# Attention and a two-layer graph convolution on one core: square-block transposes by VectorE and DMA, a Strassen form for two more groups, and half of x's operand sums later

## The chip, the cores and the metric

The kernel runs on one core of a Trainium2 chip. A core has four compute engines that run side by side: TensorE (PE, matrix products), VectorE (DVE), ScalarE (ACT) and GpSimd (POOL). A fifth, SyncE (SP), issues DMA transfers only. Each engine works through its own queue of instructions in order, and waits in it for semaphores of the others. The metric is the device time in microseconds of one execution of the whole kernel; lower is better. Beside the times there is one profiled execution, of which everything below is read.

## The reference

All is float32; there are N = 4096 nodes, x has D = 512 columns, `adj` is 4096 x 4096, the hidden width is H = 128.

```python
# layer 0: attention with adj added twice to the scores
q = x @ Wq.T + bq;  k = x @ Wk.T + bk;  v = x @ Wv.T + bv
a = q @ k.T / sqrt(D) + adj + adj
x = layernorm(x + softmax(a) @ v)
# layer 1: two graph convolutions
h = relu(adj @ (x @ W1) + b1)
out = adj @ (h @ W2) + b2
x = layernorm(x + out)
```

## The kernel before, in words

**Layer 0.** The queries are cut into NG = 8 groups of W = 512 rows, each of PER = 4 row tiles of 128. Queries and keys are never formed by themselves: with M = Wq.T Wk the scores of a group are u.T x, where u is a 512 x 512 operand of the group, made once by `u_products` (plain, sixteen products of 512 columns) or by `u_fast` (Strassen's form). For each group the 4096 keys are taken in 8 blocks d of 512. In Strassen's form after Winograd a block's scores are seven half-size products instead of eight, taken in the order 1, 2, 6, 7, 5, 4, 3 (`qk`), each of two halves j; their operands on the side of x are plain pieces of x.T or sums that were stored to DRAM (`SA`, loaded by `load_s` into the 8 slots of the pool `sap`). Two PSUM banks, X and Y, take the products, and `qk_read` (L449) adds a bank to the scores `S` on DVE: X after products 1, 6, 5, 3, Y after 2, 7, 4. The product 7 opens bank Y anew, so it must wait until DVE has read what product 2 left there. Into `S` goes beforehand a row constant (`begin_scores`, ACT) and adj, by an accumulating DMA on POOL's queue (`add_scores`, L385).

When all of a group's scores are there, they are reduced by their maximum (`shift`, L479, DVE), exponentiated (L483, ACT), summed to the denominator (L489, L492, POOL), and turned into Strassen operands (L519 and L520 on POOL, L526 and L531 on DVE). Then P x, the weights times x, follows in five ranges of key pairs with the same seven products (`px_items`, L576): 224 products a group. Their x operands `xn` are plain pieces of x, or sums of x's quarters that `sum_x` forms on POOL (L364 to L367) from rows that it loads on SP, sixteen times q, and stores as `xs_d`; for q of 2 and more it also takes two row sums of x on DVE (L408). `load_x` fetches an `xn` three phases ahead. P x is read from PSUM by `px_read` (L547 on ACT, L549 on DVE).

**The row stage.** What P x of group g - 1 gave is finished beside P x of group g and the scores of group g + 1: `row_items` (from L754) lists the steps. First V's product with P x: for groups in `FAST_V` (0 to 5) by Strassen, `rows_out_fast`, 28 products of 256 columns, with four operand sums on DVE; for groups 6 and 7 `rows_out`, 16 products of 512 columns. Then layer norm (`rows_norm`), giving the rows x1 in `XR[:, r]`, and for each tile r of 128 rows:

- `add_b2` (L732, L734): POOL adds b2 into a tile `xb`, which takes a slot of the pool `sap`, and stores it to DRAM (`x_d` in the profile) from POOL's queue, for the end of layer 1;
- `project` (L740 to L742): four PE transposes of 128 x 128 into a PSUM bank, and an ACT copy to `x1t`, of which there is one buffer (a tile of V's Strassen sums, `s3`, shares it);
- `project2` (L749, L752): four products x1 W1, and a DVE copy into `t_sb`, where all of x1 W1 is kept for layer 1.

**Layer 1** runs after that, also by Strassen, then in plain parts at the end; the change doesn't touch it.

**Order.** The order of the work is written by hand. The main loop goes through units; one has seven places, two units are a block d of the scores. At each place PE gets a product half of `qk`; hooks put there by `at(unit, place, f)` run before it; then as many steps of the unit's work list (`work[...]`) follow as their estimated PE times allow. The work list of units 33 to 48 (and so on every 16) is the row stage of group g - 1 with the products of P x of group g interleaved: `w(n)` in `row_items` stands for n products of P x. In the first units the work list holds the making of u for the groups to come, and the hooks hold the forming of x's operands, `m_sums` and `m_t3` (operands of u's Strassen form) and `sum_x`. SP's queue carries, in order of issue, the loads of `sa`, of `xn`, of `ut` and of the rows for `sum_x`; POOL's queue carries the accumulates of adj and the stores of `xs_d`, of u and of x1, each behind POOL's arithmetic.

## Time and profile before

| what | value |
|---|---|
| time, median of 3 runs (range) | 2304.09 us (2303.28 to 2306.04) |
| the profiled execution | 2308.84 us |
| its span | 2307.1 us |
| PE busy | 2276.3 us, 99% |
| DVE busy | 1617.0 us, 70% |
| POOL busy | 1018.7 us, 44% |
| ACT busy | 399.8 us, 17% |
| DMA packets, bytes | 282711, 525.14 MB |

A line of a group of instructions names the line of the kernel, the engine, the operation, output and inputs by the program's names, shapes and count, then busy time and the mean of one, then the idle time ahead of it on its engine and what ended it. Busy times of PE overlap one another, so the cost of a product is the distance from its start to the next start. In a timeline each line is a run of instructions: start, duration, engine, line; a bracket at its end gives idle time ahead and the releaser. A window's line gives start and end, length, then busy time and number of instructions of PE, PEld (the loads of PE's weights), DVE, ACT and POOL, then PE's granted clock as a share of full speed, the busy share of the DMA engines, and GB/s. Lines of DMA issues give the number, the size of one and the median time from issue to landing.

### The profile page before, as it was taken

What the parts mean: (1) busy time and instruction counts of PE and PEld (TensorE: products, weight loads), DVE (VectorE), ACT (ScalarE), POOL (GpSimd) and SP (SyncE); (2) the same over time, 40 slices, a digit from 0 to 9 for tenths busy, and PEclk for the clock granted to TensorE, in tenths of its full rate; (3) what the DMA queues carried; (4) which work ended last, traced back from release to release, by engine and by line L of the source; (5) the groups of instructions that cost most, each with busy time, mean ns of one, the idle gap of its engine ahead of it and who ended that gap; (6) DMA issues with size and microseconds to landing.
All of it is one profiled execution on the core that took longest, in us unless ns stands there. A gap on an engine that the chain in (4) does not pass through costs nothing.

```text
span 2307.1 us, 28475 instructions
## 1 busy us (share of the span) xinstructions
PE 2276.3 (99%) x10672; PEld 1750.6 (76%) x10672; DVE 1617.0 (70%) x2276; ACT 399.8 (17%) x438; POOL 1018.7 (44%) x1009
## 2 busy tenths in 40 slices
PE   9999999999999999999999999999999999999998
PEld 5888788888888888888888888888876743333456
DVE  4676776687667756765776687568657877888864
ACT  2212211131122112111311121122102000000012
POOL 3565654185327424731653274237429830001043
PEclk9999999999999999999999999999999999999999
DMA  6999878667857684777578586947754468899996
GB/s 177 273 284 309 233 215 230 193 174 215 246 135 218 189 246 114 215 213 215 151 221 232 145 218 193 259 117 210 196 191 155 155 237 321 332 347 375 352 383 218
DMA packets 282711, 525.14 MB, mean 228 GB/s; under 512 B 23184, under 2 KB 130448, under 8 KB 281680
## 3 DMA queue, kind: packets, MB, share of 16 engines
q1 hardware_dynamic: 229040, 406.12, 52.3%
q0 software_dynamic: 43296, 105.39, 20.7%
q10 hardware_dynamic: 10240, 11.82, 1.7%
q8 instruction: 85, 1.39, 0.2%
q14 instruction: 50, 0.41, 0.0%
HBM read 475.27 MB, written 46.41 MB: 226 GB/s over the span
## 4 chain that ended last, share of the span: by engine, by line
PE 92%; DVE 4%; POOL 2%; DMA 1%; issue 1%; ACT 0%; SPq 0%; POOLq 0%; DVEq 0%; ACTq 0%
PE p L576 32%; PE X L436 18%; PE b L1041 15%; PE Y L436 14%; PE v L703 3%; PE acce L1342 2%; PE psu L234 2%; PE ops L1296 1%; PE tps L749 1%; PE psu L262 1%; PE x L651 1%; PE x1ps L740 1%; DVE s L449 1%; PE psm L856 1%; DMA u_d<-uo 1%
## 5 line engine op out<-in xcount | busy, mean ns | idle before, releaser
L576 PE MATMUL p<-s,xn 128*128 128x256 f32 x3584 | 895.6, 380 | 7.0 <-DVE s L531 2.6
L576 PEld LDWEIGHTS p<-s,xn 128*128 128x128 f32 x3584 | 677.1, 190 | 111.0 <-DVE s L531 5.6
L436 PE MATMUL X<-ut,sa 128*128 128x256 f32 x1984 | 513.4, 381 | 1.7 <-DVE s L449 1.7
L492 POOL TENSOR_TENSOR lacc<-lacc,s 128x512 f32<-128x512 f32 x240 | 344.1, 1434 | 203.2 <-ACT s L483 192.3
L436 PEld LDWEIGHTS X<-ut,sa 128*128 128x128 f32 x1984 | 370.1, 190 | 64.2 <-DVE s L449 15.3
L449 DVE TENSOR_TENSOR s<-X,s 128x512 f32<-128x512 f32 x256 | 176.3, 689 | 278.6 <-PE X L436 278.2
L436 PE MATMUL Y<-ut,sa 128*128 128x256 f32 x1408 | 361.6, 380 | 0.2 <-DVE s L449 0.2
L436 PEld LDWEIGHTS Y<-ut,sa 128*128 128x128 f32 x1408 | 266.8, 190 | 37.7 <-issue 1.4
L483 ACT ACTIVATE s<-s 128x1024 f32<-128x1024 f32 x128 | 135.3, 1057 | 790.3 <-DVE s L479 790.3
L458 DVE TENSOR_TENSOR macc<-macc,s 128x512 f32<-128x512 f32 x240 | 258.1, 1075 | 1.2
L449 DVE TENSOR_TENSOR s<-Y,s 128x512 f32<-128x512 f32 x192 | 131.9, 687 | 157.0 <-PE Y L436 155.7
L479 DVE TENSOR_TENSOR s<-s,mb 128x512 f32<-128x512 f32 x256 | 231.2, 913 | 2.4 <-ACT mb L399 2.4
L385 POOL DMA_DIRECT2D s<-in_adjT_dram x64 | 84.4, 1318 | 256.7 <-ACT s L380 255.9
L549 DVE TENSOR_TENSOR ot<-p,ot 128x512 f32<-128x512 f32 x248 | 168.9, 681 | 31.4 <-PE p L576 31.2
L1008 DVE TENSOR_TENSOR tt<-ck 128x1024 f32<-128x1024 f32 x112 | 138.4, 1270 | 38.7 <-PE b L1041 33.6
L1041 PE MATMUL b<-tt,st 128*64 128x512 f32 (+1 forms) x768 | 156.0, 541 | 0.0
L380 ACT COPY s<-cb 128x2048 f32<-128x2048 f32 x64 | 121.0, 1890 | 48.1 <-PE p L576 39.8
L519 POOL TENSOR_TENSOR s<-s 128x256 f32<-128x256 f32 x128 | 124.6, 974 | 0.6
L1041 PEld LDWEIGHTS b<-tt,st 128*64 128x64 f32 x768 | 53.9, 137 | 87.8 <-issue 79.9
L526 DVE TENSOR_TENSOR s<-s 128x512 f32<-128x512 f32 x128 | 114.3, 914 | 0.0
L520 POOL TENSOR_TENSOR s<-s 128x256 f32<-128x256 f32 x128 | 107.8, 842 | 10.0
L489 POOL TENSOR_TENSOR lacc<-s 128x512 f32<-128x512 f32 x8 | 10.6, 1321 | 197.9 <-ACT s L483 197.9
(186 smaller groups left out, 2112.6 us busy)
## 6 DMA issues: line engine op xcount, KB each, us to landing
ck<-in_adjT_dram SPq DMA_DIRECT2D x128, 1024.0 KB, 7.4
s<-in_adjT_dram POOLq DMA_DIRECT2D x64, 1024.0 KB, 11.5
sa<-s_d SPq DMA_DIRECT2D x224, 256.0 KB, 5.7
xn<-in_x_dram SPq DMA_DIRECT2D x192, 256.0 KB, 4.3
xn<-xs_d SPq DMA_DIRECT2D x96, 512.0 KB, 5.7
sa<-in_xT_dram SPq DMA_DIRECT2D x168, 256.0 KB, 4.7
xn<-xs_d SPq DMA_DIRECT2D x64, 256.0 KB, 3.9
ut<-u_d SPq DMA_DIRECT2D x49, 256.0 KB, 7.2
```

Source lines behind the costliest of these rows:

```text
L380: nc.scalar.copy(s, CB[g].unsqueeze(1).to_broadcast([P, 4, W]))
L436: nc.tensor.matmul(T["X" if k in (1, 6, 5, 3) else "Y"][:, ts(j, HW)], SA[g, d, a][:, c, j, :], UT[g, b][:, c, :], start=k in (1, 2, 7) an ...
L449: nc.vector.tensor_tensor(ck, ps, ck, ALU.add)
L458: nc.vector.tensor_tensor(MACC[g], MACC[g], ck[:, h, :], ALU.max)
L479: nc.vector.tensor_tensor(ck, ck, MB[g], ALU.subtract)
L483: nc.scalar.activation(ck, ck, AF.Exp, scale=2.0)
L492: nc.gpsimd.tensor_tensor(LACC[g], LACC[g], ck[:, h, :], ALU.add)
L519: nc.gpsimd.tensor_tensor(b12, b12, b11, ALU.subtract)
L549: nc.vector.tensor_tensor(to, ps, to, ALU.add)
L576: nc.tensor.matmul(T["PX" if k in (1, 6, 5, 3) else "PY"][:, ts(f, HW)], XN[n][:, q - a, ts(f, P)], quarters(g, q)[{1: 0, 2: 2, 6: 1, 7: 0 ...
L1008: nc.vector.tensor_tensor(t[:, :2], v[:, :, 1], v[:, 0], ALU.subtract)
L1041: nc.tensor.matmul(BK[n][k][ts(half, HH)], lhs, right(u, i, half, b), start=q == 0, stop=q == NP - 1,)
```

## The change

There are five edits.

1. For groups 0 to 5, `project` gives way to three steps for each tile. `turn_blocks`: one DVE transpose of `XR[:, r]` into `x1t`, which transposes each 32 x 32 block in its place. `store_blocks`: four DMAs on SP's queue, which write `x1t` to DRAM (`xt_d`) with the blocks exchanged, in runs of 32 values. `load_blocks`: one DMA on SP's queue, which reads `xt_d` back into `XR[:, r]`, over the rows that it came from; `project2` then takes its x1 from there. The order of the row stage's steps is new, and `add_b2` comes earlier in it.
2. `FAST_V` takes in group 6. For this group alone the four operand sums are on POOL, and `project` of tile 2 comes two products of P x later.
3. u of group 1 is made by `u_fast` like those of groups 2 to 7, and their work list runs over units 1 to 15 instead of 3 to 15. `m_sums` and `m_t3` move to unit 0; one of the operands and `g_t` change places in memory.
4. `sum_x` for the sixteen q: units 0 to 15 become 0, 2, 4, 6, 8, 10, 12, 14, 15, 16, 18, 20, 21, 22, 24, 25.
5. The scores of block 1 of group 0 are begun at places 0 and 1 of unit 0 instead of 4 and 5.

```diff
+    xt_d = {
+        (g, r): dram.tile([P, ND, P], F32, name=f"xt_d{g}_{r}")
+        for g in range(NG - 2)
+        for r in range(PER)
+    }
...
-    g_t = mp.tile([P, D], F32, name="g_t")
-    ms_t = mp.tile([P, 2, 2, HW], F32, name="ms_t")
+    g_t = t_sb[:, NT - PER :, :].rearrange("p a b -> p (a b)")
+    ms_t = mp.tile([P, 3, 2, HW], F32, name="ms_t")
...
-    FAST_V = range(NG - 2)
+    FAST_V = range(NG - 1)
...
-        MV[T1] = t_sb[:, 28:32, :].rearrange("p (c a) b -> p c (a b)", c=2)
-        MV[T2], MV[T4] = (ms_t[:, n] for n in range(2))
+        MV[T2], MV[T4], MV[T1] = (ms_t[:, n] for n in range(3))
...
+        sum_ = (nc.gpsimd if g == NG - 2 else nc.vector).tensor_tensor
...
-            tt(T["s3"], a11, a21, ALU.subtract)
-            tt(a21, a21, a22, ALU.add)
+            sum_(T["s3"], a11, a21, ALU.subtract)
+            sum_(a21, a21, a22, ALU.add)
...
-                tt(a11, a21, a11, ALU.subtract)
+                sum_(a11, a21, a11, ALU.subtract)
...
-                tt(a12, a12, a11, ALU.subtract)
+                sum_(a12, a12, a11, ALU.subtract)
...
+    def turn_blocks(g, r):
+        T["x1t", g, r] = rowp.tile([P, ND, P], F32, tag="x1t", name=f"x1t{g}_{r}")
+        nc.vector.transpose(T["x1t", g, r].rearrange("p c i -> p (c i)"), XR[g][:, r, :])
+
+    def store_blocks(g, r):
+        x1t = T.pop(("x1t", g, r))
+        to = xt_d[g, r].rearrange("(b i) c (a j) -> a i c b j", i=32, j=32)
+        for a in range(4):
+            nc.sync.dma_start(
+                to[a], x1t[ts(a, 32)].rearrange("i c (b j) -> i c b j", j=32)
+            )
+
+    def load_blocks(g, r):
+        T["x1t", g, r] = XR[g][:, r, :].rearrange("p (c i) -> p c i", i=P)
+        nc.sync.dma_start(T["x1t", g, r], xt_d[g, r])
...
+        if g < NG - 2:
+            turn, store, load = (
+                lambda r, f=f: [item(0, f, g, r)] for f in (turn_blocks, store_blocks, load_blocks)
+            )
+            return [
+                *(item(0.86, rows_out_fast, g, k, j) for k in ORDER for j in range(2)),
+                *w(1), item(0, rows_last, g), *norm(2), *norm(3), *w(4), *turn(2), *w(2), *store(2),
+                *norm(0), *b2(2), *w(2), *norm(1), *w(6), *turn(3), *load(2), *b2(3), *w(2),
+                *store(3), *w(8), *turn(0), *load(3), *b2(0), *w(2), *store(0), *pro2(2), *w(8),
+                *turn(1), *load(0), *b2(1), *w(2), *store(1), *pro2(3), *w(8), *load(1), *w(2),
+                *pro2(0), *w(8), *pro2(1),
+            ]
...
-                *w(1), item(0, rows_last, g), *norm(2), *norm(3), *w(2), *pro(2), *w(2), *pro(3),
+                *w(1), item(0, rows_last, g), *norm(2), *norm(3), *w(2 + 2 * (g == NG - 2)), *pro(2), *w(2),
+                *pro(3),
...
-    work[0] = 3, [(0.86, f) for f in u_products(1)]
-    work[3] = 13, [(0.86, f) for g in range(2, NG) for f in u_fast(g)] + [(0, lambda: owing.pop()())] * 2
-    at(1, 0, m_sums)
-    at(3, 0, m_t3)
+    work[1] = 15, [(0.86, f) for g in range(1, NG) for f in u_fast(g)] + [(0, lambda: owing.pop()())] * 2
+    at(0, 0, m_sums)
+    at(0, 1, m_t3)
...
-    for q in range(NP):
-        at(max(q - 1, 0), 0, sum_x, q)
+    for q, u in enumerate((0, 2, 4, 6, 8, 10, 12, 14, 15, 16, 18, 20, 21, 22, 24, 25)):
+        at(max(u - 1, 0), 0, sum_x, q)
         for r in range(2):
-            at(q, 2 + 3 * r, lambda q, r: T["sum_x", q][0](r), q, r)
-        at(q, 6, lambda q: T["sum_x", q][1](), q)
-        at(q + 1, 2, lambda q: T["sum_x", q][2](), q)
+            at(u, 2 + 3 * r, lambda q, r: T["sum_x", q][0](r), q, r)
+        at(u, 6, lambda q: T["sum_x", q][1](), q)
+        at(u + 1, 2, lambda q: T["sum_x", q][2](), q)
...
-                at(s0 + q - early, 4, begin_scores, g, d)
-                at(s0 + q - early, 5, add_scores, g, d)
+                place = 0 if s0 + q == early else 4
+                at(s0 + q - early, place, begin_scores, g, d)
+                at(s0 + q - early, place + 1, add_scores, g, d)
```

## The prediction

> **What bounds the kernel now.** The engine totals first, then the chain that ended last:
>
> ```profile
> span 2307.1 us, 28475 instructions
> PE 2276.3 (99%) x10672; PEld 1750.6 (76%) x10672; DVE 1617.0 (70%) x2276; ACT 399.8 (17%) x438; POOL 1018.7 (44%) x1009
> ...
> PE 92%; DVE 4%; POOL 2%; DMA 1%; issue 1%; ACT 0%; SPq 0%; POOLq 0%; DVEq 0%; ACTq 0%
> ```
>
> TensorE is busy throughout and carries 92% of the chain. Every PE product taken out is worth its interval, as long as no new wait reaches PE; every wait that reaches PE costs its length. So two things are wanted: intervals, and margins. The PE timeline in a group's row stage gives the intervals (start, duration; the next start counts, since matmuls overlap):
>
> ```profile
> 473.28 0.60 PE L740 MATMUL x1ps<-ident,xr 128*128 128x128 f32 x4
> 473.71 1.03 PE L436 MATMUL Y<-ut,sa 128*128 128x256 f32 x4
> 474.58 1.03 PE L576 MATMUL p<-s,xn 128*128 128x256 f32 x4
> 475.44 1.05 PE L749 MATMUL tps<-w_t,x1t 128*128 128x128 f32 x8
> 476.33 1.03 PE L436 MATMUL X<-ut,sa 128*128 128x256 f32 x4
> ```
>
> Four transposes cost 473.71 - 473.28 = 0.43 us; two 256-column products (x4 records) 0.87, so 0.433 each; project2 0.89. By stages (window, length, busy PE, PEld, DVE, ACT, POOL, then clock, DMA share, GB/s):
>
> ```profile
> 100.00:150.00 50.00, 47.86 (x211) 40.69 (x211) 34.50 (x54) 9.45 (x16) 31.42 (x34) 0.97 1.00 269
> 280.00:320.00 40.00, 38.74 (x175) 32.58 (x175) 34.38 (x41) 6.07 (x6) 24.55 (x21) 1.00 0.89 244
> 720.00:740.00 20.00, 19.94 (x91) 16.92 (x91) 18.18 (x21) 2.85 (x2) 17.84 (x16) 1.00 0.86 249
> ```
>
> A row stage keeps DVE and POOL at 90% of 20 us with PE unhindered, so its waits are met with little to spare. The first 320 us are the only place before layer 1 with real PE losses: summing PE's start-to-start excess over each form's interval gives 10.2 us in 100 to 243, 3.8 in 243 to 320, and only 11.5 in all of 430 to 1600. DMA is full there. What a loss looks like:
>
> ```profile
> 143.77 1.13 PE L234 MATMUL psu<-xt,ms_t 128*128 128x256 f32 x4 [1.91 <-ACT uo L211]
> 144.74 1.80 PE L436 MATMUL Y<-ut,sa 128*128 128x256 f32 x4
> 146.33 1.91 PE L234 MATMUL psu<-xt,ms_t 128*128 128x256 f32 x4
> ```
>
> 1.91 us idle, then 3.4 us at half pace (granted clock 0.97 over that window): such a stall costs another 1.7 us.
>
> **What the skill says.** "TensorE: Matmul & The Clock Gate", What's actually happening: the gate goes to half rate after an idle window of about 3.4 us; the trace agrees on the 3.4 us of half pace, and shows it after 1.91 us idle already, so I charge 1.7 us to stalls near 2 us. "VectorE: DVE Perf Modes", The TRN2 errata: an f32 tensor_tensor takes (N+151)/0.96 ns, 691 at N = 512; the eviction row of the trace has 689 (L449). The three transpose paths: VectorE's transpose makes independent 32x32 blocks, so the blocks' places must be moved by something else, here the DMA. "DMA: Bandwidth & Descriptors", Specifications: under 512 B a transfer falls off the line rate, with a read-modify-write; the new stores have 128 B runs and no row of the trace has such.
>
> **The change part by part.**
>
> *1. Transposes of groups 0 to 5.* Removed: 24 sets of four transposes, 24 x 0.43 = 10.3 us of PE; with them 24 copies of 0.59 us on ACT, which idles. Added per tile: one VectorE block transpose of 128x512; four SP DMAs writing 256 KB as 2048 runs of 128 B; one SP load of 256 KB. The transpose has no row: 0.69 us by the nearest (f32 128x512, skill 0.691), up to 1.4 if it runs at half that rate, as the 128x512 rows beside POOL do (L458, 1.075); 24 x 0.69 = 16.6 us hidden in DVE's idle 10% or more, and under its floor there is no gain to bound. Issue of a DMA on SP about 0.45 us.
>
> What matters is the new order of waits. add_b2 moves ahead of most of the products of P x, since its x1 rows must be read before the load overwrites them. In every row stage (times after its first P x product, 676.74 for group 1) POOL is still working until +14.7:
>
> ```profile
> 686.13 2.95 POOL L492 TENSOR_TENSOR lacc<-lacc,s 128x512 f32<-128x512 f32 x2
> 689.04 1.18 POOL L519 TENSOR_TENSOR s<-s 128x256 f32<-128x256 f32 x1
> 690.30 1.12 POOL L520 TENSOR_TENSOR s<-s 128x256 f32<-128x256 f32 x1
> ...
> 706.38 1.77 POOL L732 TENSOR_TENSOR xb<-xr,b_t 128x512 f32<-128x512 f32 x1
> 708.45 0.63 POOL L734 DMA_DIRECT2D x_d<-xb  x1 [0.30 <-POOL xb L732]
> ```
>
> I laid the new order out by its intervals. (a) add_b2 of tile 2 runs +14.9 to +16.4; the load of tile 2 sits on SP from +9.5 and holds SP until then. Its own store's landing is long past. (b) Behind it on SP: the next operand `sa` takes the slot of xb_2 and waits for the x1 store (x_d), issued +16.7 and landing 2.3 to 4.4 later when not behind the accumulate, so +19.4; then an `xn` load; then store 3's four DMAs, +20.4 to +21.75. (c) The transpose of tile 0 needs the single x1t buffer that store 3 reads, so on DVE it waits for store 3's landing, L after the last issue. DVE comes to it at about +19.5. (d) Behind it on DVE, in order: the transpose 0.6, a subtraction of the maximum 0.6, a P x read 0.6, a small copy 0.21, another subtraction 0.6, and the read of bank Y 0.69 (start to start), 3.3 in all. The product k = 7 of block 2 restarts bank Y at +27.3 and needs that read. So PE stalls 21.75 + L + 0.1 + 3.3 - 27.3 = L - 2.1 us.
>
> L has no row. From below: 2.3, the fastest x1 store, all of 2 KB runs: no stall. From above: the store of c, 2 KB in 4 B runs, lands 9.8 after issue (`c_d`): stall 7.7. Packets' times in the trace go 159 ns for 4 KB, 85 for 2 KB, 46 for 1 KB, 27 for 512 B, so I estimate 13 for 128 B; 128 of them per DMA engine in a tile is 1.7 us beside traffic at 0.86, about 3.2 to 3.5 with the fixed part. I take L = 3.4, a stall of 1.3 without the clock's half pace: 6 x 1.3 = +8.0 us. Later steps have slack: tile 1 is loaded by about +38 and is used at +49.0. An `sa` has a median of 15.6 us between landing and use (minimum 4.4), an `xn` 4.7 (minimum 0.1), so a hold of SP of 7 us can show through the `xn` too; that is in L's upper cases.
>
> *2. u of group 1 by Strassen.* 16 products of 512 columns at 0.866 against 28 of 256 at 0.433: 13.86 - 12.12 = -1.73 us. Its m_sums and m_t3 move to the start of unit 0: three POOL subtractions ahead of POOL's accumulates, one DVE behind T1; first read a unit later, so nothing, and 2 us if POOL holds DVE there.
>
> *3. Rows of group 6.* The same arithmetic, -1.73 us; four operand sums on POOL, about 1.5 us each, not DVE's 0.6. The PE product k = 6 needs the sum after k = 2: the reads of P x end at 1719.0 in before, plus 3 x 1.5 = 1723.5, and PE is there at 1722.0. Before has a stall of 0.95 us at the same place (1723.10), so +0.8 us net.
>
> *4. Half of x's sums later.* Sixteen times: a load of 512 KB on SP, two DVE row sums of 0.86 (L408; the eight moved all have them), four POOL sums of 0.87 (L364 to L367), a store of 512 KB on POOL's queue. Eight leave units 0 to 13 and land in units 15 to 25. They relieve 8 MB of traffic in a stretch at DMA share 1.00, where 14.0 us of PE are lost in all to waits of this sort; they add two DVE sums to units where DVE has 34.38 of 40 us. The upper bound on the gain is about 9 (most of the 10.2 between 100 and 243), the loss up to 4 (one more such stall with its half clock). I take -2. P x of the first block needs sums 0 to 3 first, still in units 0 to 6; the last sum (unit 25) is read over ten units later.
>
> *5. Bias and scores of block 1 begun four places earlier.* One ACT fill of 1.89 and an accumulate of 1 MB at the start of unit 0; hidden by ACT's idleness, 0; uncovered it would hold the adj buffer only.
>
> Sum: -10.3 - 1.73 - 1.73 = -13.8 of PE; +8.0 + 0.8 - 2 = +6.8 of waits; -7.0. The profiled execution took 2308.84 (1.7 us outside its span), so it would take 2301.8; it lies 4.75 over the median of the runs, 2304.09, hence 2297.1.
>
> **Rivals.** *Hidden.* The stores land fast enough (L = 2.3) and nothing stalls: 2297.1 - 8.0 = **2289**. For it: DVE idles 10% and x1 stores land in 2.3 to 4.4. Against: the chain (a) to (d) has no slack. *The start gives nothing:* sums land where DVE is at 86%, and the stalls of 100 to 243 come from u's stores (the chain has `u_d`, 1%): start 0 to +4 in place of -2, **2299 to 2303**. *Slower: 128 B runs land late.* Place: store 3 in each of six row stages. Without stalls the sum is 2289.1; slower than 2308.7 it is from 19.6 / 6 = 3.3 us a group, that is L - 2.1 + 1.7 from L = 3.7 if the half pace follows, 5.4 if not. At L = 6: 6 x (3.9 + 1.7) = 33.6, **2322.7**; at 7, 2329. For it: the read-modify-write, the 9.8 of `c_d`, and 49,152 packets into traffic at 0.86. Against: each DMA engine has but 128 packets per tile, and the `c_d` packets themselves took 9 ns each.
>
> **How the numbers follow.** Main case 0.40 (2291 to 2303), hidden 0.20, start without gain 0.15, slower 0.25. Faster: 0.33 of main, 0.20, 0.05; same: 0.07, 0.10 and 0.02 of the late-landing case where it is just past break-even; slower 0.23. About 0.2% (4.6 us) is what a measurement can tell from no change. The range 2286 to 2322 leaves out the lowest of the hidden case with a full gain at the start, and L over 6.
>
> **What would show it.** PE's records fall by the 24 x 4 transposes and its busy time by 10 to 14 us. In each row stage, DVE's transpose of the third tile waits on a DMA of xt_d and the read of Y after it is late, with PE idle about 1.3 us near +27; the load of tile 2 waits on POOL's xb. The landing of the small stores is L. PE's excess in 100 to 243 falls from 10.2 to about 8. The prediction is wrong if the landing is beyond 4 us, if POOL reaches add_b2 much later than +14.9, or if the start moves by more than 4 us.

## The result, and the profile after

The changed kernel takes 2354.38 us (median of 4, 2354.04 to 2355.11) against 2304.28 us of the kernel before: 1.0215 times as long, 95% interval 1.0203 to 1.0227. The prediction was 2297 us, with a range from 2286 to 2322. Line numbers are higher in the changed kernel: the scores' products are L441 (L436 before), their reads L454 (L449), the subtraction of the maximum L484 (L479), the running maximum of the scores L463 (L458), POOL's denominator sums L497 (L492), the Strassen operands of P x L524, L525 on POOL and L531, L536 on DVE (L519, L520, L526, L531), P x itself L581 (L576). The page of the changed kernel, its totals and the chain that ended last:

```profile
span 2352.8 us, 28577 instructions
PE 2281.1 (97%) x10624; PEld 1764.3 (75%) x10624; DVE 1614.4 (69%) x2307; ACT 388.9 (17%) x418; POOL 1018.8 (43%) x1008
...
PE 83%; DVE 8%; DMA 4%; POOL 2%; issue 2%; SPq 0%; ACT 0%; DVEq 0%; POOLq 0%; ACTq 0%
```

The chain has moved from PE (92% before) to DVE (4 to 8%) and DMA (1 to 4%): PE waits. Where it waits is read from the starts of the first P x product of each group: 462.69, 676.74, 891.13, 1105.06, 1319.51, 1533.47 and 1733.50 for groups 1 to 7 before; 461.1, 684.1, 906.8, 1127.7, 1350.9, 1571.6 and 1779.9 after. The start is 1.6 us shorter, what follows the last row stage 0.7 us; as the profiled execution of before lies 4.6 us above its median, neither can be told from nothing. The six row stages between are 48.0 us longer, about 8 each, although each has lost 1.72 us of transposes.

The PE timeline in one of them (start, duration; in brackets idle time ahead and what ended it), then DVE's and POOL's and SP's at the same place:

```profile
697.36 1.10 PE L581 MATMUL p<-s,xn 128*128 128x256 f32 x4
702.80 1.22 PE L581 MATMUL p<-s,xn 128*128 128x256 f32 x2 [4.34 <-DVE s L536]
703.82 1.91 PE L441 MATMUL X<-ut,sa 128*128 128x256 f32 x4
```

```profile
701.53 0.71 DVE L756 STREAM_TRANSPOSE x1t<-xr 128x512 f32<-128x512 f32 x1 [2.54 <-DMA xt_d<-x1t]
702.17 0.58 DVE L536 TENSOR_TENSOR s<-s 128x256 f32<-128x256 f32 x1
```

```profile
690.38 1.34 POOL L390 DMA_DIRECT2D s<-in_adjT_dram  x1
```

```profile
690.29 3.57 SPq L762 DMA_DIRECT2D xt_d<-x1t  x4
```

PE waits for the DVE sum L536, the last operand after product 7 of the first range of P x. On DVE that sum stands behind the transpose of tile 3, which waits 2.54 us for the one x1t buffer, that is for the store of tile 2. That store was issued on SP at the very moment at which POOL issued the 1 MB accumulate of adj. What the profile says of the store's four DMAs, and of those of the next tile, 15 us later:

```profile
L762 SPq DMA_DIRECT2D xt_d<-x1t x4: 575/620/1610, 690.3 to 692.3; - x4
...
  DVE x1t L756: 2.5, 1
...
DMA to landing us min/median/max: 2.3/7.3/9.4
```

```profile
L762 SPq DMA_DIRECT2D xt_d<-x1t x4: 575/631/635, 704.9 to 706.9; - x4
...
DMA to landing us min/median/max: 3.6/3.8/4.2
```

Away from the accumulates, the last part of such a store (that of tile 3) lands 2.2 to 4.2 us after its issue; beside the accumulate it takes 9.2 us here. In the trace's packets, 506 of 128 B go in the first microsecond of the store; once the accumulate's 2 KB packets run, 187 small ones go in three microseconds beside 294 large. The small packets take turns with packets of some 0.17 us each. "DMA: Bandwidth & Descriptors", Queues, rings and completion order, in the Trainium skill says that an engine alternates between its queues by packets; the counts agree in kind. (It puts a packet at 9 to 17 descriptors; in this trace the records of 128 B come singly, one about every 0.16 us between those of the accumulate.)

Every stage shows this stall (4.5 to 5.2 us by starts, ahead of P x product number 18), and a second, near +45 us after the first P x product, of 2.1 us (3.2 in the first stage), again for L536, ahead of number 44. Around each of the first and four of the six second ones PE goes at half pace: the mean granted clock is 0.989 (0.998 before). The windows that answer to those shown of before (window, length, busy PE, PEld, DVE, ACT, POOL, clock, DMA share, GB/s):

```profile
100.00:150.00 50.00, 50.00 (x231) 43.48 (x231) 32.12 (x50) 10.28 (x18) 24.21 (x26) 1.00 0.93 253
280.00:320.00 40.00, 37.02 (x170) 31.77 (x169) 37.12 (x48) 6.41 (x6) 34.65 (x33) 1.00 0.98 288
726.00:746.00 20.00, 18.04 (x83) 15.41 (x82) 13.74 (x21) 2.11 (x2) 9.94 (x9) 0.91 0.86 246
```

Half of the sums of x did leave the stretch 100 to 150 (PE 47.86 to 50.00, DMA share 1.00 to 0.93), and POOL's work grew in 280 to 320 (24.55 to 34.65), where PE lost (38.74 to 37.02).

### The profile page after: what moved, and what is told of

Same layout as the page of the kernel before. It is cut to its first block, busy times and chain, and to the rows that moved or that the text cites. A ratio compares the mean times of both kernels' runs of the same rounds, so it can differ in the third digit from the quotient of the medians.

```text
span 2352.8 us, 28577 instructions
## 1 busy us (share of the span) xinstructions
PE 2281.1 (97%) x10624; PEld 1764.3 (75%) x10624; DVE 1614.4 (69%) x2307; ACT 388.9 (17%) x418; POOL 1018.8 (43%) x1008
## 4 chain that ended last, share of the span: by engine, by line
PE 83%; DVE 8%; DMA 4%; POOL 2%; issue 2%; SPq 0%; ACT 0%; DVEq 0%; POOLq 0%; ACTq 0%
PE p L581 27%; PE X L441 16%; PE b L1079 14%; PE Y L441 12%; PE psu L239 3%; PE v L710 3%; PE acce L1381 2%; DMA xt_d<-x1t 2%; DVE s L484 1%; DVE s L531 1%; PE ops L1335 1%; DVE macc L463 1%; PE tps L774 1%; DVE s L536 1%; DVE s L454 1%
## 5 line engine op out<-in xcount | busy, mean ns | idle before, releaser
L581 PE MATMUL p<-s,xn 128*128 128x256 f32 x3584 | 907.4, 383 | 50.2 <-DVE s L536 45.3
L581 PEld LDWEIGHTS p<-s,xn 128*128 128x128 f32 x3584 | 683.5, 192 | 157.1 <-DVE s L536 52.8
L441 PE MATMUL X<-ut,sa 128*128 128x256 f32 x1984 | 522.6, 387 | 3.0 <-DVE s L454 3.0
L441 PEld LDWEIGHTS X<-ut,sa 128*128 128x128 f32 x1984 | 379.6, 194 | 66.3 <-DVE s L454 14.0
L497 POOL TENSOR_TENSOR lacc<-lacc,s 128x512 f32<-128x512 f32 x240 | 344.7, 1436 | 185.4 <-ACT s L488 174.7
L454 DVE TENSOR_TENSOR s<-X,s 128x512 f32<-128x512 f32 x256 | 176.5, 689 | 302.5 <-PE X L441 297.9
L441 PE MATMUL Y<-ut,sa 128*128 128x256 f32 x1408 | 360.7, 379 | 1.0 <-DVE s L454 1.0
L441 PEld LDWEIGHTS Y<-ut,sa 128*128 128x128 f32 x1408 | 266.4, 190 | 37.0 <-DVE s L454 1.4
L454 DVE TENSOR_TENSOR s<-Y,s 128x512 f32<-128x512 f32 x192 | 132.1, 688 | 197.3 <-PE Y L441 197.1
L463 DVE TENSOR_TENSOR macc<-macc,s 128x512 f32<-128x512 f32 x240 | 230.0, 958 | 1.2
L484 DVE TENSOR_TENSOR s<-s,mb 128x512 f32<-128x512 f32 x256 | 223.6, 878 | 0.7 <-ACT mb L404 0.7
L524 POOL TENSOR_TENSOR s<-s 128x256 f32<-128x256 f32 x128 | 122.7, 959 | 0.6
L531 DVE TENSOR_TENSOR s<-s 128x512 f32<-128x512 f32 x128 | 116.4, 933 | 0.0
L525 POOL TENSOR_TENSOR s<-s 128x256 f32<-128x256 f32 x128 | 108.4, 847 | 10.0
```

The source lines that it names most:

```text
L441: nc.tensor.matmul(T["X" if k in (1, 6, 5, 3) else "Y"][:, ts(j, HW)], SA[g, d, a][:, c, j, :], UT[g, b][:, c, :], start=k in (1, 2, 7) an ...
L454: nc.vector.tensor_tensor(ck, ps, ck, ALU.add)
L463: nc.vector.tensor_tensor(MACC[g], MACC[g], ck[:, h, :], ALU.max)
L484: nc.vector.tensor_tensor(ck, ck, MB[g], ALU.subtract)
L497: nc.gpsimd.tensor_tensor(LACC[g], LACC[g], ck[:, h, :], ALU.add)
L524: nc.gpsimd.tensor_tensor(b12, b12, b11, ALU.subtract)
```

## The experiments

Times are medians; each ratio is to the kernel before on the same chip. Where P x products are numbered, they count from the group's first (0 to 223). The expectations name their theories by letters, A to F.

### Which part costs, and is it the store?

Edit 1 of the change, called part 1 here, undone (the condition of the new list made false):

```diff
-        if g < NG - 2:
+        if False:
```

> The changed kernel with part 1 alone undone: groups 0 to 5 keep project on TensorE and the order of steps that the kernel before has; parts 2 to 5 stay. Theory (the loss lies in the six row stages alone, +48.0 us between the starts of P x of groups 1 and 7): 2302 us, that is 2304.3 less 1.6 before the first row stage and 0.7 after the last. Rival (later sums or u of group 1 delay something that the row stages meet): 2315 or more.

Measured: 2306.80 us, 1.0007 (0.9999 to 1.0015). The whole loss is part 1, and parts 2 to 5 together give nothing that can be measured. (The 2302 expected took over the gains at the start and the end from the profiled execution of before; the six row stages together are 1271.2 us, 1270.8 before.) This run is the base for what follows: 2306.8, or 2306.8 - 10.3 = 2296.5 with the transposes gone and nothing waiting. Against that the changed kernel waits 57.9 us.

Three ways to mend the first stall. Long runs:

```diff
-            nc.sync.dma_start(
-                to[a], x1t[ts(a, 32)].rearrange("i c (b j) -> i c b j", j=32)
-            )
+            nc.sync.dma_start(xt_d[g, r][ts(a, 32)], x1t[ts(a, 32)])
```

> The changed kernel with the same four stores per tile at the same places, but each writes its 32 rows as they lie, in runs of 2 KB; the blocks are then not exchanged, so x1 W1 is formed from other values. Theory (runs of 128 B take turns packet by packet with the 1 MB accumulate of adj that is issued at the same moment, so the store of tile 2 lands 9.1 us after its last issue; 2 KB runs are sixteen times fewer packets): that store lands within 4 us, the transpose of tile 3 does not hold DVE, the stall of 5.0 us with its half pace goes in all six stages, about 2354 - 6 x 7.2 = 2311 us. Rival (any store behind the accumulate lands late, whatever its runs): 2350 to 2356.

The transpose of tile 3 put off:

```diff
-                *norm(0), *b2(2), *w(2), *norm(1), *w(6), *turn(3), *load(2), *b2(3), *w(2),
-                *store(3), *w(8), *turn(0),
+                *norm(0), *b2(2), *w(2), *norm(1), *w(6), *load(2), *b2(3), *w(4), *turn(3), *w(2),
+                *store(3), *w(4), *turn(0),
```

> The changed kernel with the transpose of tile 3 four products of P x later, which puts it behind the DVE sums (L536) that product 7 of P x waits for; the load of tile 2 and the stores of tile 2 stay where they are. Theory (the wait for the single x1t buffer at the head of DVE's queue is what holds PE): the stall of 5.0 us goes, about 2311 us. Rival (SP, held by the load of tile 2 until its store has landed, makes the operands behind it late): the stall stays or turns into a wait for sa or xn, 2335 to 2356.

Tile 2 stored earlier:

```diff
-                *norm(3), *w(4), *turn(2), *w(2), *store(2),
+                *norm(3), *turn(2), *w(2), *store(2), *w(4),
```

> The changed kernel with the transpose and the stores of tile 2 four products of P x earlier, so that the stores are issued about 3 us before the accumulate. Theory (the store is late only because the accumulate's packets share the DMA engines with it): it lands before +9 us, the transpose of tile 3 does not wait, the stall of 5.0 us goes, about 2311 us. Rival (128 B runs land late by themselves): they still take 7 us or more to land, and 2335 or more.

Measured: 2345.37 (1.0174, 1.0161 to 1.0188), 2363.49 (1.0253, 1.0239 to 1.0267), 2348.44 (1.0187, 1.0172 to 1.0203). None came near 2311, and the second is slower than the changed kernel. Yet the store of tile 2 was read rightly. It is shown here with 2 KB runs, still issued with the accumulate, and then with 128 B runs, issued before it:

```profile
L761 SPq DMA_DIRECT2D xt_d<-x1t x4: 318/413/428, 906.6 to 907.9; - x4
...
DMA to landing us min/median/max: 1.6/1.7/3.6
```

```profile
L762 SPq DMA_DIRECT2D xt_d<-x1t x4: 576/621/627, 908.2 to 910.1; - x4
...
DMA to landing us min/median/max: 2.2/2.2/2.3
```

Both land within 3.6 us (over all stages, within 4.1 with long runs). But 2 KB runs are no safeguard by themselves: 96 of their 128 packets had started before the accumulate's first one. In the same run and stage the store of tile 1, also of 2 KB runs, is issued some 3 us after the second accumulate, behind loads on SP:

```profile
L761 SPq DMA_DIRECT2D xt_d<-x1t x4: 482/656/1010, 935.1 to 937.4; - x4
...
DMA to landing us min/median/max: 8.1/8.6/9.7
```

The stall near +14 fell from 5 us to 1.6 with long runs (2.2 in one stage), to 1.5 when stored earlier. But the second grew. In the run with long runs, then in that with the earlier store:

```profile
939.95 1.13 PE L581 MATMUL p<-s,xn 128*128 128x256 f32 x4 [0.18 <-DVE s L531]
945.22 1.22 PE L581 MATMUL p<-s,xn 128*128 128x256 f32 x2 [4.15 <-DVE s L536]
```

```profile
949.61 1.22 PE L581 MATMUL p<-s,xn 128*128 128x256 f32 x2 [4.14 <-DVE s L536]
```

A wait of 2.1 us by starts in the changed kernel is 4.3 us here (3.4 in one stage); that the first stall had given DVE time to catch up is a likely reading, not a shown one. DVE's wait for the buffer had not gone, either: in all three runs it moved to the next transpose, that of tile 0, which the prediction had named, with 2.0 to 4.2 us in these two. With the transpose put off it was 5.6 to 6.8 us there, as the stores of tile 3 then stood only four products ahead of it; PE waited in many places (for xn, for the bank Y, for POOL) and again 4.3 us at the end. Whether this wait is the reason for the second stall is asked next.

### Is it the transposes, the transfers or the order?

Transposes and order kept, stores and loads out:

```diff
-        to = xt_d[g, r].rearrange("(b i) c (a j) -> a i c b j", i=32, j=32)
-        for a in range(4):
-            nc.sync.dma_start(
-                to[a], x1t[ts(a, 32)].rearrange("i c (b j) -> i c b j", j=32)
-            )
...
-        nc.sync.dma_start(T["x1t", g, r], xt_d[g, r])
```

> The changed kernel with its VectorE transposes and its order of steps, but without the stores and loads of xt_d: project2 takes the rows as they lie, so x1 W1 is formed from other values. Theory A (the second stall, 4.3 us at about +40 in each stage where the first is mended, comes from DVE standing still for the single x1t buffer, 2.7 us at about +25, that is from the landing of store 3): nothing stands still, DVE keeps up, the ten microseconds of transposes come through: about 2298 us (2306.8 less 10.3, with 1 or 2 us of small stalls). Theory B (DVE is simply full between +26 and +46, with POOL slowing its sums to 1.2 to 1.75 us, and the transposes are too much): the stall stays above 3 us, 2320 or more.

Stores and loads kept, transposes out:

```diff
-        T["x1t", g, r] = rowp.tile([P, ND, P], F32, tag="x1t", name=f"x1t{g}_{r}")
-        nc.vector.transpose(T["x1t", g, r].rearrange("p c i -> p (c i)"), XR[g][:, r, :])
+        T["x1t", g, r] = XR[g][:, r, :].rearrange("p (c i) -> p c i", i=P)
```

> The changed kernel with its stores and loads, but without the VectorE transposes: the stores read the rows themselves, x1 W1 is formed from other values. No x1t buffer is waited for on DVE. Theory A (all loss comes by way of DVE's wait for that buffer): about 2298 us. Theory C (the transfers and the loads that hold SP make xn and sa late by themselves): 2315 or more, with PE waiting for DMA or with reads late behind sa.

The order alone, on TensorE:

```diff
-            turn, store, load = (
-                lambda r, f=f: [item(0, f, g, r)] for f in (turn_blocks, store_blocks, load_blocks)
-            )
+            turn = store = lambda r: []
+            load = pro
```

> The changed kernel with its order of steps (add_b2 early), but with the transposes on TensorE and an ACT copy back into the rows, in the place of each load; no stores, no loads, no DVE transposes. Theories A and C: the order itself costs nothing, 2307 us as with the old order. Theory D (POOL's early add_b2, while DVE has its sums, is what makes DVE late): a stall of 3 us or more near +40 in each stage, 2325 or more.

Measured: 2341.61 (1.0155, 1.0139 to 1.0170), 2331.03 (1.0111, 1.0098 to 1.0125), 2349.41 (1.0191, 1.0177 to 1.0205). The first two reject theory A: the second stall is 2.7 to 4.3 us without one wait for the buffer, and 2.6 to 4.3 us without a transpose on DVE. The last shows the largest part: without stores, loads or transposes on DVE, the order costs 42.6 of the 57.9 us. The runs of the transposes and of the transfers alone, which carry the same order, therefore say nothing for theories B or C by themselves.

Of the 42.6 us some 8 are of this run's own making. In it ACT copies each turned tile back into the rows, which add_b2 on POOL must have read; a read of P x stands behind that copy, and PE waits for it, 8.0 us in six stages. ACT, then PE:

```profile
922.53 0.58 ACT L752 COPY xr<-x1ps 128x512 f32<-128x512 f32 x1 [1.69 <-POOL xb L739]
```

```profile
923.65 0.70 PE L581 MATMUL p<-s,xn 128*128 128x256 f32 x2 [1.34 <-ACT ot L552]
```

The run of the transfers alone has no such copy; it lies 2331.03 - 2296.5 = 34.5 us over the base without transposes, with its stores and loads in that. So the order's own part is some 34 us or less, still the largest. Its stall in the run of the order alone comes two products earlier than in the changed kernel (number 42, not 44). PE first, then DVE, then POOL:

```profile
945.41 1.03 PE L581 MATMUL p<-s,xn 128*128 128x256 f32 x4
950.27 1.22 PE L581 MATMUL p<-s,xn 128*128 128x256 f32 x2 [3.83 <-DVE s L531]
```

```profile
944.59 1.75 DVE L484 TENSOR_TENSOR s<-s,mb 128x512 f32<-128x512 f32 x1
946.26 2.29 DVE L463 TENSOR_TENSOR macc<-macc,s 128x512 f32<-128x512 f32 x1
948.48 1.74 DVE L531 TENSOR_TENSOR s<-s 128x512 f32<-128x512 f32 x1
```

```profile
944.08 1.71 POOL L739 TENSOR_TENSOR xb<-xr,b_t 128x512 f32<-128x512 f32 x1
946.71 2.97 POOL L497 TENSOR_TENSOR lacc<-lacc,s 128x512 f32<-128x512 f32 x2
```

DVE is not waiting. Its three sums take 1.7 to 2.3 us where an undisturbed one takes 0.6 from start to start, while POOL works beside them for nearly all of that time.

Of the order, what? Only add_b2 moved:

```diff
-                *w(1), *norm(0), *w(1), *pro2(2), *norm(1),
+                *w(1), *norm(0), *w(1), *pro2(2), *b2(2), *norm(1),
...
-                *pro2(0), *w(4), *pro2(1), *w(2), *b2(2), *w(4), *b2(3), *w(4), *b2(0), *w(4), *b2(1),
+                *pro2(0), *b2(3), *w(4), *pro2(1), *w(6), *b2(0), *w(10), *b2(1),
```

> Groups 0 to 5 transpose on TensorE at the old places (as the run with part 1 undone, 2306.8 us); only add_b2 of the four tiles comes early, after 7, 15, 25 and 35 products of P x instead of 21, 25, 29 and 33. Theory E (in the new order P x runs ahead of the hooks that prepare its operands, because the PE work of the row stage was taken out from between its first products or put off): add_b2's place is harmless, 2305 to 2310 us. Theory D (POOL's early add_b2 makes DVE late): 2325 or more.

Only project and project2 put off:

```diff
-                *w(1), item(0, rows_last, g), *norm(2), *norm(3), *w(2), *pro(2), *w(2), *pro(3),
...
+                *w(1), item(0, rows_last, g), *norm(2), *norm(3), *w(5), *norm(0), *w(1), *norm(1),
+                *w(14), *b2(2), *w(2), *pro(2), *w(2), *b2(3), *w(2), *pro2(2), *w(2), *b2(0), *w(4),
+                *b2(1), *pro(3), *w(4), *pro2(3), *w(6), *pro(0), *w(4), *pro2(0), *w(4), *pro(1), *w(4),
+                *pro2(1),
```

> Groups 0 to 5 transpose on TensorE and keep add_b2 at its old places, but project and project2 come late, project2 at the places of the changed kernel (27, 37, 47 and 55 products of P x instead of 7, 11, 15 and 19). The first products of P x then follow one another as closely as in the changed kernel. Theory E: PE waits 3 us or more for the DVE sum (L536) behind product 7 of the second range of P x in each stage, 2330 to 2352 us. Theory D: 2305 to 2310.

Measured: 2313.08 (1.0034, 1.0021 to 1.0047) and 2331.89 (1.0115, 1.0099 to 1.0130). add_b2 alone costs 6.3 us, a little over what theory E allowed; putting off the PE work costs 25.1. The two add to 31.4, not far from the 34 us at most that are the order's own; the places of these two runs are not exactly those of the changed kernel, so the difference says nothing. With the PE work gone from between them, the first P x products follow one another sooner: number 16 stands at +21.6 us in the kernel before and at +13.0 after.

### Is it the pace, or POOL beside DVE?

The changed kernel with the old pace, by empty steps that count 0.44 and 0.9 us in the interleaving:

```diff
+            short, long = [(0.44, lambda: None)], [(0.9, lambda: None)]
+            pro2 = lambda r: [item(0, project2, g, r)]
...
+                *w(2), *short, *w(2), *short, *turn(2), *w(2), *store(2), *norm(0), *b2(2), *long,
...
```

> The changed kernel, whole, with one thing added: empty steps in groups 0 to 5 that count in the interleaving like the old project and project2 (0.44 and 0.9 us, at the old places), and project2 itself counted as nothing, so that P x takes the places beside the scores that it has in the kernel before. Theory E: the stall behind product 7 of the second range goes or falls under 1.5 us; what the single x1t buffer costs stays: 2297 to 2325 us. If pace has no part in it: 2345 or more.

The same, with the steps spread by where stores land:

```diff
+                *norm(3), *turn(2), *w(2), *store(2), *norm(0), *short, *w(2), *short, *w(1), *norm(1), *w(1),
+                *b2(2), *long, *w(2), *turn(3), *store(3), *short,
...
+                *w(4), *turn(0), *long, *b2(0), *w(2), *store(0),
...
```

> As the run before, and the transposes are put where the stores of the tile before have landed: tile 2 at once and stored ahead of the first accumulate, tile 3 stored within it with nothing behind it for ten products of P x, tile 0 between the accumulates, tile 1 last; loads after their stores' landing. Theory E with the buffer's part: both stalls go, 2306.8 - 10.3 = 2296.5 us, up to 2303. If DVE cannot take the transposes here: over 2315.

Measured: 2342.82 (1.0159, 1.0142 to 1.0176) and 2331.71 (1.0115, 1.0100 to 1.0131). Both miss what theory E allowed (up to 2325 and up to 2303), though they are 11.6 and 22.7 us faster than the changed kernel. Neither settles the question. In the first, DVE still waits 2.5 to 3.4 us for the buffer at tile 3, and PE waits for DVE in several places. In the second no transpose waits for the buffer, and in the first 56 products no wait for a DVE sum is above 0.9 us, as theory E had it. In their place stands a stall of 3.3 us in each stage. ACT, then PE:

```profile
908.93 0.81 ACT L644 ACTIVATE xr<-xr,shift,rstd 128x512 f32<-128x512 f32 x1 [6.34 <-POOL shift L693]
```

```profile
910.32 0.67 PE L581 MATMUL p<-s,xn 128*128 128x256 f32 x2 [3.13 <-POOL lacc L497]
```

The norm of tile 0, which this run takes earlier, waits on ACT for POOL. Behind it on ACT is the read of P x (909.65 to 910.21) that frees PE's bank, so this read, and not the POOL sum that the view names, is the likely releaser. With the half pace after it, this stall is about all that a stage of 217 to 220 us has over the 212 to 213 to be had. What the old pace and these places are worth without it was not tried. Pace alone is therefore neither shown nor ruled out as a remedy.

Next, POOL was relieved: all but the first of a group's denominator sums left out, once with the order alone, once with the changed kernel, once with the old order as their base:

```diff
-            for h in range(2):
-                nc.gpsimd.tensor_tensor(LACC[g], LACC[g], ck[:, h, :], ALU.add)
+            pass
```

> The new order on TensorE (2349.4 us), with the denominators' sums on POOL (L497) left out but for the first pair of each group, so that rows are divided by another number. Theory F (in the first 56 products of P x DVE is full, because its sums of two SBUF operands take 1.1 to 1.7 us instead of 0.6 beside POOL's; taking PE work out of that stretch or putting it off only shows it): with POOL relieved the stalls go, 2307 us or less. If DVE is late for want of its own time or by the order alone: 2335 or more.

> The changed kernel with the same sums left out. Theory F: of the 57.9 us of waiting (2354.4 against 2306.8 - 10.3 = 2296.5) what comes from DVE's and POOL's sharing goes, what comes from the transpose of tile 3 behind the store of tile 2 stays at most at 5.4 and 1.7 us a stage: 2297 to 2339 us. If POOL's load has no part: 2350 or more.

> The old order with TensorE's transposes (2306.8 us) with the same sums of POOL left out: the base for the two runs without these sums. Theory F: POOL had cost the old order nothing in the row stages, so it gains only what POOL costs at the start and at the end; 2292 to 2297 us, no more than 3 us from the new order without sums (2294.7). If the new order costs something of its own: 2288 or less.

Measured: 2294.74 (0.9955, 0.9940 to 0.9970), 2303.46 (0.9995, 0.9987 to 1.0003), 2298.81 (0.9975, 0.9963 to 0.9987), the last a little over what was expected. With POOL relieved the new order, 42.6 us slower than the old one with these sums, is no slower (4.1 us faster by the medians; the intervals overlap). Its six row stages take 1271.6 us together, as much as those of the kernel before (1270.8); ACT's wait for add_b2 has gone too. The windows of the first 56 P x products say how (the kernel before, the order alone, the order alone without these sums):

```profile
891.10:946.70 55.60, 55.23 (x277) 48.19 (x277) 43.68 (x63) 18.32 (x21) 45.06 (x45) 1.00 0.66 180
```

```profile
906.20:969.60 63.40, 58.23 (x277) 50.19 (x276) 48.92 (x63) 18.16 (x21) 47.61 (x48) 0.95 0.64 174
```

```profile
886.30:942.50 56.20, 55.24 (x278) 48.22 (x277) 39.96 (x63) 18.17 (x21) 27.16 (x34) 1.00 0.72 197
```

The same 63 DVE instructions take 43.68, 48.92 and 39.96 us. Which of them change, in the groups of DVE over these stretches, in the same sequence of kernels (count, then busy time and mean ns):

```profile
L479 DVE TENSOR_TENSOR s<-s,mb 128x512 f32<-128x512 f32 x13 | 13.4, 1044 | 0.0
...
L449 DVE TENSOR_TENSOR s<-Y,s 128x512 f32<-128x512 f32 x6 | 4.1, 684 | 3.1 <-PE Y L436 3.1
```

```profile
L484 DVE TENSOR_TENSOR s<-s,mb 128x512 f32<-128x512 f32 x13 | 15.5, 1192 | 0.0
...
L454 DVE TENSOR_TENSOR s<-Y,s 128x512 f32<-128x512 f32 x6 | 4.1, 684 | 3.1 <-PE Y L441 3.1
```

```profile
L484 DVE TENSOR_TENSOR s<-s,mb 128x512 f32<-128x512 f32 x13 | 10.7, 821 | 0.0
...
L454 DVE TENSOR_TENSOR s<-Y,s 128x512 f32<-128x512 f32 x6 | 4.1, 689 | 3.4 <-PE Y L441 3.3
```

The sum of two SBUF operands swings from 821 to 1192 ns; the read of a PSUM bank, of the same shape, stays at 684 to 689. The Trainium skill's "GPSIMD Engine Reference", 1. Specifications, has the rule (GpSimd shares its SBUF interfaces with VectorE, against instructions with two SBUF inputs); these rows are its size in this kernel. The instruction times in the trace of the kernel before show it sum by sum. Of 375 sums of DVE on record in L479 and L458 between the first P x of group 1 and of group 7, the 192 that no arithmetic of POOL overlaps take 677 to 693 ns. The 90 that it overlaps for six tenths of their time or more take 1451 on average. All 513 reads of a PSUM bank (L449, L549) take 672 to 693, whatever POOL does. What the runs don't tell apart is how much of the kernel's loss comes by this sharing and how much by POOL's own operands for P x (L524, L525), which stand behind its sums and so come sooner as well.

In the changed kernel without the sums the buffer's wait is left by itself. DVE, then PE:

```profile
901.93 0.71 DVE L755 STREAM_TRANSPOSE x1t<-xr 128x512 f32<-128x512 f32 x1 [2.05 <-DMA xt_d<-x1t]
```

```profile
903.00 0.70 PE L580 MATMUL p<-s,xn 128*128 128x256 f32 x2 [2.29 <-DVE s L535]
```

Its price follows: 2303.5 against 2294.7 - 10.3 = 2284.4 is 19.1 us, 3.2 a stage, for transposes and transfers together; the executions of this run spread from 2299.0 to 2314.5. In the whole kernel this part is 57.9 - 42.6 = 15.3 by the order alone, and 8.0 more if that run's own wait is taken off its 42.6; so 15 to 23 us.

### The sums of x

> Groups 0 to 5 transpose on TensorE in the old order (as the run with part 1 undone, 2306.8 us), and part 4 is undone too: the sixteen sums of x are back in units 0 to 15. If the later sums give or take nothing: 2305 to 2308.5 us. If they gave the 2 us that the prediction took: 2309. If they cost 2 us, and hid what the Strassen forms of u and of the rows saved: 2303.

```diff
-    for q, u in enumerate((0, 2, 4, 6, 8, 10, 12, 14, 15, 16, 18, 20, 21, 22, 24, 25)):
+    for q, u in enumerate(range(NP)):
```

Measured, on top of part 1 undone: 2305.55, 1.0000 (0.9992 to 1.0008), where part 1 undone alone has 2306.80. The later sums give nothing. PE's excess over its intervals, summed as in the prediction, in the run with part 1 undone: 7.8 us in 100 to 243 (10.2 before), but 7.2 in 243 to 430 (4.6 before). With the old sums it is 9.0 and 4.6. The later sums moved the stalls.

### Can the transposes be had elsewhere?

Everything after the norms from 60 P x products on, with empty steps in the old places:

```diff
+                *w(4), *long, *w(41), *turn(2), *w(2), *store(2), *w(2), *b2(2), *w(12), *load(2), *turn(3),
...
```

> The changed kernel with the old pace of P x in its first 20 products (empty steps, as in the run with the old pace), and everything that follows the norm late: transposes, stores, add_b2, loads and project2 from 60 products of P x on, spread so that each transpose comes after the store before it has landed. Theory F: the first 56 products have no DVE transposes, no add_b2 and no x1t buffer to wait for, but PE lacks 5.4 us of other work there; DVE needs about 43 of the 50 us left: small stalls, 2297 to 2309 us. If DVE needs all of the PE work that stood there: 2315 or more.

Measured: 2314.04 (1.0032, 1.0021 to 1.0044). Groups 1 to 4 take 214.6, 213.9, 214.1 and 213.9 us from P x to P x, as before (214.4, 213.9, 214.5, 214.0): the saved 1.72 us are waited away. Group 0's stage takes 221.4, of which PE waits 4.74 for one load of xt_d; that stage alone is 7.4 us over its 214.0, as the whole run is 7.2 over its base. The run misses the 2297 to 2309 expected.

Then project2 in the next group's stage, so that PE has real work between the first P x products again, for groups 1 to 5; and for groups 1 to 4 with loads issued sooner:

```diff
+                *norm(3), *fetch(2), *w(2), *short, *w(2), *short, *w(1), *norm(0), *w(1), *pro2p(2), *fetch(3),
...
+                *w(41), *turn(2), *w(2), *store(2), *w(2), *b2(2), *w(12), *turn(3),
...
```

> Group 0 transposes on TensorE as before; groups 1 to 5 by VectorE and DMA from 60 products of P x on, and their project2 only in the next group's row stage, at the old places of project2, from a load of xt_d into the x1t buffer. The first products of P x thus keep 3.6 of the 5.4 us of other PE work between them. 20 tiles save 8.7 us of PE. Theory F: stalls of 3 to 6 us in all (group 1's stage has none of that work), 2306.8 - 8.7 + 4 = 2302 us, up to 2306. If the transposes make DVE late in the later ranges as well: over 2310.

```diff
+                *norm(3), *fetch(2), *w(2), *short, *w(2), *pro2p(2), *fetch(3), *w(1), *norm(0), *short,
...
```

> As the run with project2 in the next group's stage, but for groups 1 to 4 alone (group 5 on TensorE; group 4's project2 after group 5's own), and the loads of xt_d issued before the accumulate or long ahead of their project2, since there PE had waited 2.4 to 3.1 us for such a load in each stage. 16 tiles save 6.9 us of PE. Theory F: 2306.8 - 6.9 + 2 = 2302 us, 2299 to 2304, the first version faster than the kernel before. If the later transposes still make DVE late: 2306 or more.

Measured: 2316.47 (1.0048, 1.0035 to 1.0061) and 2308.51 (1.0014, 1.0007 to 1.0020). In the first, PE waits 1.4 to 3.0 us a stage for the loads, and the last project2 of group 5 falls behind the sums that layer 1 takes of x1 W1, so these lack it, and the end is 9.9 us longer. In the second, the middle stages at last gain; one of them (from P x to P x), and the same one of before:

```profile
1097.40:1309.30 211.90, 211.55 (x998) 185.10 (x997) 152.78 (x214) 39.99 (x37) 97.72 (x92) 1.00 0.77 209
```

```profile
1105.10:1319.50 214.40, 213.97 (x1013) 186.43 (x1012) 148.94 (x210) 42.16 (x41) 99.15 (x92) 1.00 0.71 196
```

2.5 us (2.0 and 2.7 in its neighbours), PE busy 211.55 of 211.90. It is lost again in group 5's stage, 12.6 us longer than in the base. That stage does group 4's project2 as well (3.6 us), and PE waits there for its load:

```profile
1565.85 2.07 PE L774 MATMUL tps<-w_t,x1f 128*128 128x128 f32 x8 [5.12 <-DMA x1f<-xt_d]
```

The six stages together take 1271.3 us, the base 1271.2. No version faster than the kernel before by what a measurement can tell, with the whole work done, was found; one with this load mended was not tried.

## Why the prediction was wrong

**The bound, and what a PE product is worth.** Right where PE alone sets the pace, as the 2.0 to 2.7 us a stage above show (1.72 are the transposes; PE's excess over its intervals fell a little as well); wrong for the first 56 P x products. I read 18.18 of 20 us on DVE as "little to spare" and went on to price DVE's and POOL's rows as fixed. They are not: a DVE sum's price depends on what POOL does beside it. The prediction had a row "beside POOL" at 1.075 and used it only as an upper case for the transpose, whose price POOL did not change.

**Step 1, the operations.** The transpose was taken at 0.69 us; its 24 take 0.695 to 0.714. The estimate of 13 ns for a packet of 128 B is the median of the trace, and the landing of store 3, taken as 3.4 us after its last issue, is 2.2 to 4.2. (Six times 1.3 is 7.8, not 8.0, which changes nothing.)

**Step 1 (a), "Its own store's landing is long past".** Failed. Store 2 is issued at +6.2 to +8.1, the accumulate at +6.3, where it stands in the trace of before too, with 9.1 to 10.2 us to its landing. I let it weigh on the x1 stores only. Store 2 lands at +16.4 to +17.3. So the wait for the x1t buffer comes at tile 3 and not at tile 0, ahead of L536 and not of the read of Y, in a stall of 5 us where the sum has 1.3. (Once store 2 was mended, the wait at tile 0 did come.) Between 15 and 23 us of the loss are this and the other new operations.

**Step 1, the new order.** The failed term that weighs most, and it had no line in the sum: it was put at nothing without a reason. I "laid the new order out by its intervals" and used that only to time the waits. P x number 16 comes at +13.0 where it came at +21.6, so the same DVE and POOL work must be done sooner, beside less PE work. That was not priced: 42.6 us in the run of the order alone on TensorE, some 34 without that run's own wait on ACT, and nothing once POOL's sums are left out. The rivals held no such case; "the chain (a) to (d) has no slack" looked at a few instructions of DVE, not at its load.

**Steps 2 and 4.** -1.73 and -2 were forecast for the start; parts 2 to 5 together give +1.6 us (-0.2 to +3.5 by the ratio's interval). The rival that the start gives nothing was right.

**Step 3.** -0.9 forecast (its own figures, 1723.5 - 1722.0 against 0.95, make the added wait 0.6 rather than 0.8); from P x of group 6 to that of group 7 it is 200.0 us before, 199.9 with part 1 undone, in one profiled execution each. A gain, if any, of a tenth.

**The rivals.** The slower one named the right mechanism, small runs late beside other traffic, at the wrong store, and at L = 7 gave 2329; but the store at its real place, with all other new operations, accounts for 15 to 23 of the 57.9 us. That its 2329 lies nearest to the result is luck.

## What to carry to other kernels

A stage in which the bounding engine is unhindered can still be held up by two others that are nearly full. Before taking work off the bounding engine there, ask whether its work was the time in which the others caught up, and test the new order alone, without the new operations. Look in such a test for waits that it brings itself. Where VectorE and GpSimd work side by side on SBUF operands, price a sum by a row with the same neighbour, and make GpSimd's work cheaper first. A store's landing depends on what other queues send at that moment: look up what is issued in the microseconds around it.

## What was not expected of the hardware

- A store in 128 B runs is not slow by itself (2.2 us from issue to landing for 64 KB); issued together with the 1 MB accumulate it takes 9.2. With 2 KB runs at the same place it takes 3.6 to 4.1 at most, but 8.1 to 9.7 where the accumulate's packets already run and loads stand ahead of it.
- DVE's 128x512 sum of two SBUF operands has a mean of 821 ns in the stretch with POOL busy 27 of 56 us, 1044 with 45 of 56, and 1192 with 48 of 63. POOL's share of the last is no higher than of the second, so the share of a stretch does not set the price; which instructions overlap does.
- Leaving out POOL's denominator sums, two of 1.43 us per pair of key tiles, makes the whole kernel 6 us faster with the old order (2298.8 against 2304.8) though POOL was busy for 44% of it only. The gain lies before and after the row stages, which together are 5.0 us longer in that run's profile than in the kernel before.
